# A hybrid of scans, convolutions, attention and expert mixtures on one core: experts' outputs added by way of ScalarE and GpSimd, decays issued two at a time

## The chip, the core and the metric

The kernel runs on one core of a Trainium2 chip. The core has five engines that each work through their own instructions in order: TensorE (PE in the profile) for matrix products, VectorE (DVE), ScalarE (ACT), GpSimd (POOL), and SyncE (SP), which here issues DMAs. Engines wait for each other through semaphores. The metric is the time of one execution on the device in microseconds (us); lower is better.

## What is computed

Four layers work on an input of 4 images of 32x32 positions (1,024 positions) and 256 channels. Layer 0 is a convolution and then a state-space scan with 512 channels of 64 states; layer 1 is a small residual convolution block; layer 2 is masked attention and a mixture of 8 experts; layer 3 is a second scan, with 512 channels of 16 states, and a second mixture of 8 experts. Cut to the parts that the change touches:

```python
# the scans, layers 0 and 3: for each image, channel and state, over the positions
dA = jnp.exp(dtt[:, :, None] * A)
h = dA * h + (dtt * xt)[:, :, None] * Bt[:, None, :]
y = jnp.einsum('bdn,bn->bd', h, Ct)

# the mixture of layer 2 (hidden size 256; layer 3 has 512 and no residual inside)
for e in range(E):
    h = jax.nn.gelu(tokens @ w1[e] + b1[e], approximate=False)
    y = h @ w2[e] + b2[e]
    out = out + combine[:, e:e + 1] * y
```

`combine` holds each token's weights for the experts; it is zero but for the best two. All eight experts are computed for all tokens.

## The kernel before

Two streams of work are interleaved as the program is written. One is the list of scans (`scans`, line 378). A scan of one image is cut into units: one unit is 128 rows (pairs of a channel and a state) by 1,024 positions. Layer 0 has 256 units for an image and layer 3 has 64, so there are 1,280 units, in the order of the list `SCANS` (line 31): (layer 0, image 0), (0,1), (3,0), (0,2), (3,1), (0,3), (3,2), (3,3).

For unit k these steps run:

- `load` (line 460): a DMA broadcasts the step sizes into a tile dA; there are five such tiles.
- `decay` (line 473): ScalarE turns dA into exp(scale x dA) in place, with the row's A as the scale.
- `first` (line 483): two matmuls spread the inputs into a PSUM tile ps_rep, of which there are two.
- VectorE multiplies ps_rep by B in place (line 542), and then runs the scan over the positions into a tile h (line 546).
- GpSimd multiplies h by C (line 547).
- `pair` (line 498): TensorE sums over the states of two units into ps_y.

In the loop at line 533, `load` runs four units ahead, `decay` two and `first` one.

The other stream is the side work: stages named `front` (the start of layer 0), `middle` (the end of layer 0, layers 1 and 2, and the start of layer 3) and `last` (the end of layer 3), one of each for each image. They are generators that give up control after each small step. After each half of a unit the loop in `run` (line 607) lets up to two side steps go. It stops when the clock of some engine has passed that of VectorE: the kernel keeps a clock for each engine, and adds an estimate for every instruction that it writes (`Metered`, line 96). So side work is written beside as many scan units as it takes VectorE's clock to follow. A stage also waits where it needs the result of a scan. The other way round, a scan needs what a stage makes: where that isn't there five units before the scan begins, `need` (line 556) writes out all that is missing at once. The last scan, (3,3), begins at unit 1216, and its inputs come from the last `middle`, so what is left of that stage at unit 1211 comes in one block that no scan stands beside.

The mixture is `moe` (line 582). Its items run through `pipe` (line 194), which gives each item its first step at one tick and its second step at the next. Items are of two kinds. An "h" item multiplies tokens by a part of the first weights into a PSUM tile ps_h, and ScalarE applies the gelu with a bias into h_m, one tick later. An "o" item multiplies h_m by the second weights into a PSUM tile ps_e for two blocks of 128 tokens, and one tick later VectorE adds the result, scaled by the token's weight, to the running sum tb: two `scalar_tensor_tensor` of 128x256 for an item, 32 items and so 64 instructions for a mixture. The PSUM tiles of the side work, ps_h and ps_e among them, share three buffers in turn (`ps`, line 188). The gelu and the exponential of a decay lie in different tables of ScalarE, and each switch is an instruction of its own, ACT_TABLE_LOAD.

Attention (`heads`, line 449) goes in 64 steps for an image: scores into PSUM, their exponentials on ScalarE into p, and the products with the values. In the block that no scan stands beside, the scores go to the scans' free PSUM tiles under the name ps_sx.

Line 128 in the profile is the helper of `Metered` that writes most instructions, so groups are told apart there by their tiles.

Of the kernel before, what the change touches and what calls it, by code (L numbers as in the profile page):

```python
# [7 lines left out]
F32 = mybir.dt.float32  # L8
BF16 = mybir.dt.bfloat16
I32 = mybir.dt.int32  # L10
AF = mybir.ActivationFunctionType
ALU = mybir.AluOpType
# [4 lines left out]
P = 128  # L17
NB = 4
L = 1024
TB = L // P  # L20
C = 256
# [115 lines left out]
class Hybrid:  # L137
# [240 lines left out]
    def scans(self, mp, psum):  # L378
# [7 lines left out]
        nc = self.nc  # L386
# [10 lines left out]
        y = None  # L397
# [44 lines left out]
        def chunks_ahead(k, late=False):  # L442

            if not late and k + AHEAD < len(units) and units[k + AHEAD][2:] == (0, 0, 0):
                waiting.append(k + AHEAD)
            while waiting:
                scan, d = units[waiting[0]][:2]
                if ("parts", *scan, d) not in self.ready:  # L450
                    if waiting[0] - k > LATEST:
                        break
                    if not late:
                        return True
                    self.alone = True
                chunk(waiting.pop(0))
                self.alone = False
            return False

        def load(k):  # L460
            if k >= len(units):
                return
            scan, d, c, i, j = units[k]
            n = self.states[scan[0]]
            G = P // n
            a = mp.tile([P, L], F32, tag="dA", name="dA", bufs=5)
            r = 64 * c + 32 * j + G * i
            nc.sync.dma_start(
                a, self.mem["dt", *scan, d][r : r + G, :].unsqueeze(0).to_broadcast([n, G, L])
            )  # L470
            state[k] = a

        def decay(k):
            if k >= len(units):
                return
            scan, d, c, i, j = units[k]
            G = P // self.states[scan[0]]
            col = (d * P + 64 * c + 32 * j) // G + i
            nc.scalar.activation(
                state[k], state[k], AF.Exp, scale=self.tables[scan[0]][0][:, col : col + 1]  # L480
            )

        def first(k):
            if k >= len(units):
                return
            scan, d, c, i, j = units[k]
            spread = self.tables[scan[0]][1]
            G = P // self.states[scan[0]]
            ps = psum.tile([P, L], F32, tag="x", name="ps_rep", bufs=2)
            for g in range(2):  # L490
                cols = slice(g * 512, (g + 1) * 512)
                nc.tensor.matmul(
                    ps[:, cols], lhsT=spread[:, i, :], rhs=chunks[scan, d][:, 2 * c + j, cols],
                    start=True, stop=True,
                )
            state[k] = (state[k], ps)

        def pair(k):

            nonlocal y  # L500
            scan, d, c, i, j = units[k]
            n = self.states[scan[0]]
            per = 32 * n // P
            collect = self.tables[scan[0]][2]
            if i == 0:
                y = psum.tile([P, 512], F32, tag="y", name="ps_y", bufs=1)
            h = [state.pop(k - 1), state.pop(k)]
            for g in range(2):
                for j in range(2):
                    at = 32 * (2 * g + j)  # L510
                    nc.tensor.matmul(
                        y[at : at + 32, :], lhsT=collect[:, i, :],
                        rhs=h[j][:, g * 512 : (g + 1) * 512],
                        start=(i == 0), stop=(i == per - 1), tile_position=(0, at),
                    )
            if i == per - 1:
                yo = mp.tile([P, 512], F32, tag="yo", name="yo", bufs=2)
                nc.scalar.copy(yo, y)
                to = self.keep(("y", *scan, d, c), [64, L])
                for g in range(2):  # L520
                    nc.sync.dma_start(to[:, g * 512 : (g + 1) * 512], yo[64 * g : 64 * g + 64, :])
                if c == 1:
                    self.done.add((scan, d))
# [4 lines left out]
        for k in range(2, 4):  # L528
            load(k)
        decay(0)  # L530
        decay(1)
        first(0)
        for k in range(len(units) + 4):
            waits = chunks_ahead(k)
            load(k + 4)
            if not waits:
                first(k + 1)
            decay(k + 2)
            if k < len(units):
                a, inp = state.pop(k)  # L540
                B, Cm = rows[units[k][0]]
                nc.vector.tensor_tensor(inp, inp, B, ALU.mult)
            yield
            if k < len(units):
                h = mp.tile([P, L], F32, tag="h", name="h", bufs=5)
                nc.vector.tensor_tensor_scan(h, a, inp, 0.0, ALU.mult, ALU.add)
                nc.gpsimd.tensor_tensor(h, h, Cm, ALU.mult)
                state[k] = h
            if k % 2 == 1 and 2 <= k < len(units) + 2:
                pair(k - 2)  # L550
            if waits:
                chunks_ahead(k, True)
                first(k + 1)
            yield
# [1027 lines left out]
    def moe(self, which, b, tb):  # L1582

        nc, tc, a = self.nc, self.tc, self.a
# [5 lines left out]
        with tc.tile_pool(name=f"m{which}{b}", bufs=1, side="right") as op:  # L1590
            xT = op.tile([P, 2, L], F32, name="xTm")
            cw = op.tile([P, TB, NEXP], F32, name="cw")
# [9 lines left out]
            with tc.tile_pool(name=f"mg{which}{b}", bufs=1, side="right") as gp:  # L1602
# [4 lines left out]
                ps = self.ps("ps_lg", (P, TB, NEXP))  # L1607
# [14 lines left out]
                if which == 2:  # L1622
                    for j in range(0, TB, 2):
                        tj = tb[:, j : j + 2, :]
# [15 lines left out]
                got = {}  # L1640
# [13 lines left out]

                yield from self.pipe(range(TB // 2), last, add, cost=1.0)

            hidden_of = {}
            got = {}

# [24 lines left out]
            def two(item):  # L1684
                kind, e, g, i = item
                if kind == "h":
                    nc.scalar.activation(
                        hidden_of[e, g][:, i, :], got.pop(item), AF.Gelu,
                        bias=b1[:, e * KH + i : e * KH + i + 1],
                    )  # L1690
                    return
                ps = got.pop(item)
                for s in range(2):
                    m = 4 * g + 2 * i + s
                    nc.vector.scalar_tensor_tensor(
                        tb[:, m, :], ps[:, s, :], cw[:, m, e : e + 1], tb[:, m, :],
                        ALU.mult, ALU.add,
                    )

            items = []  # L1700
            blocks = [(e, g) for e in range(NEXP) for g in range(2)]
            for n in range(len(blocks) + 1):
                if n < len(blocks):
                    items += [("h", *blocks[n], i) for i in range(KH)]
                if n:
                    items += [("o", *blocks[n - 1], i) for i in range(2)]
            yield from self.pipe(items, one, two, cost=2.6 if which == 2 else 3.4)

    def route(self, gp, lg, cw, renorm):

# [296 lines left out]
```

## Time and profile before

| what | value |
|---|---|
| time, median of 3 runs | 6460.27 us (6456.73 to 6466.56) |
| the profiled execution: time | 6467.21 us |
| the profiled execution: span from first to last instruction | 6465.4 us |
| mean TensorE clock granted | 0.825 |

```profile
PE 5210.1 (81%) x20249; PEld 2107.8 (33%) x20249; DVE 5153.1 (80%) x4328; ACT 3408.1 (53%) x4075; POOL 3648.4 (56%) x1796
```

The line gives each engine's busy time, its share of the span, and its instructions; PEld is TensorE's loading of weights, which overlaps its products. These are averages over stretches of very different kinds. The largest groups of ScalarE and GpSimd, and ScalarE's table loads, follow. A row has the line, engine, operation and tiles, the shapes, the count, then busy time and mean ns of one, and then the engine's idle time ahead of these instructions with what ended most of it.

```profile
L128 POOL TENSOR_TENSOR h<-h,rows 128x1024 f32<-128x1024 f32 x1280 | 3026.7, 2367 | 1816.9 <-DVE h L128 1567.0
L128 ACT ACTIVATE dA<-dA,A_L_conv_A_log 128x1024 f32<-128x1024 f32 x1024 | 1147.7, 1144 | 616.5 <-DMA dA<-dt 575.9
L128 ACT ACT_TABLE_LOAD x483 | 619.7, 1283 | 58.4 <-PE ps_h L128 43.1
L128 ACT ACTIVATE h_m<-ps_h,cols 128x512 f32<-128x512 f32 x384 | 260.2, 687 | 507.7 <-PE ps_h L128 505.2
```

A further 95 table loads stand under line 266, which makes 578.

### The profile page before, as it was taken

The page shows a single profiled execution, that of the slowest core. Times are in us where ns is not written, and L with a number is a line of the kernel's source. Part 1 is how long each engine was busy: PE and PEld are TensorE (multiplying, and loading weights), DVE is VectorE, ACT ScalarE, POOL GpSimd, SP SyncE. Part 2 cuts the span into 40 slices and gives each one's busy share as a digit, 9 for nine tenths or more (in the row PEclk, how much of TensorE's full clock was granted, in tenths as well). Part 3 has the DMA queues.
Part 4 walks back from the last instruction along what each step waited for, and adds up shares of the span by engine and source line. Part 5 has one row for each costly group of instructions (what it writes and reads, how often), then busy time and mean ns, then how long its engine had stood idle before and what let it go on. Part 6 is the DMA issues. An engine that isn't in the chain of part 4 may idle for free. (4 is left out here: it accounts for less than half of the span.)

```text
span 6465.4 us, 59678 instructions
## 1 busy us (share of the span) xinstructions
PE 5210.1 (81%) x20249; PEld 2107.8 (33%) x20249; DVE 5153.1 (80%) x4328; ACT 3408.1 (53%) x4075; POOL 3648.4 (56%) x1796
## 2 busy tenths in 40 slices
PE   6677685689797579989689689798699688968979
PEld 2222130222342022243245232253254222524656
DVE  5888989988898998899889988898899981258311
ACT  3565664355576335567568445477387353246311
POOL 2797868665557666555856665557756661065100
PEclk7677695689797579989789689798699788978979
DMA  3555546443355566345644665354555750156221
GB/s 114 162 158 174 176 154 198 158 147 116 125 182 174 169 163 163 114 137 178 193 150 165 189 158 142 107 168 163 178 169 168 193 146 7 53 154 159 64 69 33
DMA packets 347995, 935.77 MB, mean 145 GB/s; under 512 B 37444, under 2 KB 119952, under 8 KB 346064
## 3 DMA queue, kind: packets, MB, share of 16 engines
q1 hardware_dynamic: 345248, 929.36, 47.2%
q0 software_dynamic: 2128, 2.13, 0.2%
q8 instruction: 166, 2.72, 0.2%
q14 instruction: 165, 1.35, 0.1%
q10 hardware_dynamic: 288, 0.20, 0.0%
HBM read 841.81 MB, written 93.16 MB: 145 GB/s over the span
## 5 line engine op out<-in xcount | busy, mean ns | idle before, releaser
L128 POOL TENSOR_TENSOR h<-h,rows 128x1024 f32<-128x1024 f32 x1280 | 3026.7, 2367 | 1816.9 <-DVE h L128 1567.0
L128 DVE TENSOR_TENSOR_SCAN h<-dA,ps_rep 128x1024 f32<-128x1024 f32 x1280 | 2923.0, 2284 | 142.8 <-ACT dA L128 12.8
L128 DVE TENSOR_TENSOR ps_rep<-ps_rep,rows 128x1024 f32<-128x1024 f32 x1280 | 1550.9, 1212 | 182.6 <-PE ps_rep L128 178.4
L128 ACT ACTIVATE dA<-dA,A_L_conv_A_log 128x1024 f32<-128x1024 f32 x1024 | 1147.7, 1144 | 616.5 <-DMA dA<-dt 575.9
L128 PE MATMUL ps_rep<-S,spread_L_conv_A_log 96*128 96x512 bf16 x2048 | 770.4, 465 | 840.8 <-DVE h L128 791.1
L128 PE MATMUL ps_y<-h,collect_L_conv_A_log 128*32 128x512 f32 x4096 | 739.5, 773 | 14.6 <-POOL h L128 14.6
L128 PE MATMUL ps_h<-xTm,we 128*128 128x512 f32 x1536 | 716.5, 606 | 0.0
L128 PE MATMUL ps_e<-we,h_m 128*128 128x256 f32 x3072 | 701.2, 381 | 2.5 <-ACT h_m L128 1.7
L128 PEld LDWEIGHTS <-spread_L_conv_A_log 96*128 96x128 bf16 x2048 | 159.3, 103 | 1651.4 <-DVE h L128 1348.1
L128 ACT ACT_TABLE_LOAD x483 | 619.7, 1283 | 58.4 <-PE ps_h L128 43.1
L128 PEld LDWEIGHTS ps_e<-we,h_m 128*128 128x128 f32 x3072 | 579.2, 190 | 153.6 <-issue 62.7
L128 DVE SCALAR_TENSOR_TENSOR tb<-ps_e,cw,tb 128x256 f32<-128x256 f32 x512 | 220.1, 474 | 410.6 <-PE ps_e L128 410.5
L128 ACT ACTIVATE h_m<-ps_h,cols 128x512 f32<-128x512 f32 x384 | 260.2, 687 | 507.7 <-PE ps_h L128 505.2
L128 ACT ACTIVATE p<-ps_sc 128x512 f32<-128x512 f32 x432 | 234.4, 595 | 382.8 <-PE ps_sc L128 381.9
L128 PEld LDWEIGHTS ps_h<-xTm,we 128*128 128x128 f32 x1536 | 292.4, 193 | 333.4 <-issue 287.8
L128 ACT ACTIVATE dA<-dA,A_L_attn_A_log 128x1024 f32<-128x1024 f32 x256 | 290.6, 1146 | 198.3 <-DMA dA<-dt 168.8
L128 PE MATMUL ps_rep<-S,spread_L_attn_A_log 96*128 96x512 bf16 x512 | 182.7, 444 | 178.6 <-DVE h L128 167.7
L128 PE MATMUL ps_at<-p,v 128*32 128x512 f32 x1024 | 276.6, 621 | 0.9 <-ACT sums L128 0.7
L128 PE MATMUL ps_at<-p,ones 128*32 128x512 f32 x1024 | 276.5, 620 | 0.0
L128 PE MATMUL ps_sc<-qT,kT 32*128 32x512 f32 x864 | 262.6, 665 | 14.8 <-ACTq L1382 8.8
L128 POOL TENSOR_TENSOR sp_l<-sp_l,sp_e 128x512 f32<-128x512 f32 x62 | 78.4, 1265 | 272.4 <-DVE sp_e L128 250.5
L128 PE MATMUL ps_cv<-pad,diag 128*128 128x512 f32 x504 | 230.9, 599 | 0.0
(333 smaller groups left out, 4926.2 us busy)
## 6 DMA issues: line engine op xcount, KB each, us to landing
dA<-dt SPq DMA_DIRECT2D x1280, 512.0 KB
we<-in_L_ffn_W_dram SPq DMA_DIRECT2D x64, 512.0 KB
parts<-parts SPq DMA_DIRECT2D x62, 384.0 KB
S<-parts SPq DMA_DIRECT2D x93, 256.0 KB
dt<-sp_r SPq DMA_DIRECT2D x64, 256.0 KB
y<-yo SPq DMA_DIRECT2D x128, 128.0 KB
y_back<-y SPq DMA_DIRECT2D x64, 256.0 KB
we<-in_L_ffn_w_dram SPq DMA_DIRECT2D x64, 256.0 KB
```

What stands on the lines that cost most here:

```text
L128: return got(*args, **kw)
```

## The change

In five of the eight mixtures, those of layer 2 for images 0 to 2 and those of layer 3 for images 0 and 1, the addition of an expert's output is done in two steps. ScalarE scales each 128x256 half out of PSUM into a new tile y_m in SBUF (two buffers), and at the next tick of `pipe` GpSimd adds the whole 128x512 tile to tb. The three mixtures that are left keep the addition on VectorE. The price that is given to `pipe` for a tick stays the same.

In the loop over units, the decays of units k+1 and k+2 are written together at each even k, ahead of `first`; before, the decay of unit k+2 was written at each k, behind `first`.

```diff
         decay(0)
-        decay(1)
         first(0)
         for k in range(len(units) + 4):
             waits = chunks_ahead(k)
             load(k + 4)
+            if k % 2 == 0:
+                decay(k + 1)
+                decay(k + 2)
             if not waits:
                 first(k + 1)
-            decay(k + 2)
...
+            beside = b < (NB - 1 if which == 2 else NB - 2)
             hidden_of = {}
             got = {}
...
                 ps = got.pop(item)
+                if beside:
+                    got[item] = y = op.tile([P, 2, C], F32, tag="ym", name="y_m", bufs=2)
                 for s in range(2):
                     m = 4 * g + 2 * i + s
+                    if beside:
+                        nc.scalar.activation(y[:, s, :], ps[:, s, :], AF.Copy, scale=cw[:, m, e : e + 1])
+                        continue
                     nc.vector.scalar_tensor_tensor(
                         tb[:, m, :], ps[:, s, :], cw[:, m, e : e + 1], tb[:, m, :],
                         ALU.mult, ALU.add,
                     )
+
+            def three(item):
+                kind, e, g, i = item
+                if kind == "h":
+                    return
+                m = 4 * g + 2 * i
+                tj = tb[:, m : m + 2, :]
+                nc.gpsimd.tensor_tensor(tj, tj, got.pop(item), ALU.add)
...
-            yield from self.pipe(items, one, two, cost=2.6 if which == 2 else 3.4)
+            steps = (one, two, three) if beside else (one, two)
+            yield from self.pipe(items, *steps, cost=2.6 if which == 2 else 3.4)
```

## The prediction

> **What bounds the kernel now.** I read the page's 40 slices first, then busy time by stretch, VectorE's groups and waits, and the order of VectorE and ScalarE inside a mixture. Durations are of the profiled execution (6467.2 us, span 6465.4), which lies 7 us above the median of 6460.3; I sum against it and subtract those 7 at the end.
>
> ```profile
> DVE  5888989988898998899889988898899981258311
> PEclk7677695689797579989789689798699788978979
> ```
>
> For 33 of 40 slices VectorE is 80 to 100% busy; then it falls to 1 and 2. By stretch (the first and fourth rows are mixtures of layer 2 and layer 3 beside full scans, then attention beside scans, almost pure scan, the solo burst, and all until the burst):
>
> ```profile
> core 0: us, PE busy (x) PEld busy (x) DVE busy (x) ACT busy (x) POOL busy (x), PEclk, DMA share, GB/s
> 1718.00:1872.00 154.00, 150.27 (x600) 81.38 (x598) 145.37 (x140) 122.15 (x116) 82.52 (x35) 0.98 0.47 151
> ...
> 3293.00:3609.00 316.00, 307.87 (x1258) 163.99 (x1257) 300.53 (x226) 260.27 (x246) 190.59 (x81) 0.99 0.49 162
> ...
> 1302.00:1718.00 416.00, 352.68 (x1756) 106.48 (x1757) 354.26 (x293) 211.79 (x302) 241.49 (x114) 0.85 0.38 126
> 2083.00:2351.00 268.00, 157.65 (x528) 34.34 (x521) 257.64 (x175) 83.57 (x77) 175.66 (x76) 0.56 0.59 176
> 5331.00:5695.00 364.00, 329.73 (x1324) 154.99 (x1322) 64.88 (x170) 116.56 (x162) 20.89 (x16) 0.92 0.09 30
> 0.00:5331.00 5331.00, 4230.32 (x16643) 1572.61 (x16645) 4755.41 (x3780) 3010.62 (x3569) 3397.96 (x1657) 0.81 0.52 159
> ```
>
> Up to 5331 us the scan's VectorE work sets the pace: one unit is a multiply and a scan, and in the timeline of a plain stretch a unit returns every 3.54 us (2199, 2202.5, 2206.0). The mixtures are nearly balanced: VectorE 95%, TensorE 97%, ScalarE 80%. That matters, since the change only relieves the first. VectorE's groups until 5331:
>
> ```profile
> L128 DVE TENSOR_TENSOR_SCAN h<-dA,ps_rep 128x1024 f32<-128x1024 f32 x1212 | 2767.8, 2284 | 135.4 <-ACT dA L128 11.2 <-DVE ps_rep L128 3.4 <-DVEq L1382 1.0
> L128 DVE TENSOR_TENSOR ps_rep<-ps_rep,rows 128x1024 f32<-128x1024 f32 x1212 | 1468.6, 1212 | 173.8 <-PE ps_rep L128 169.6
> L128 DVE SCALAR_TENSOR_TENSOR tb<-ps_e,cw,tb 128x256 f32<-128x256 f32 x320 | 136.2, 471 | 14.7 <-PE ps_e L128 14.6
> ```
>
> Decays are hardly ever late (11 us), and exactly 320 expert additions lie here. From 5331 VectorE idles because the last scan, (3,3), needs layer 2 and front of image 3. That is the solo burst: TensorE paces it, with an attention step every 2.81 us (rows of ScalarE's timeline):
>
> ```profile
> 5344.78 1.02 ACT L128 ACTIVATE p<-ps_sx 128x1024 f32<-128x1024 f32 x1 [1.78 <-PE ps_sx L128]
> 5347.59 1.02 ACT L128 ACTIVATE p<-ps_sx 128x1024 f32<-128x1024 f32 x1 [1.78 <-PE ps_sx L128]
> ```
>
> After 6025 us TensorE alone runs the last mixtures, which keep the old code.
>
> **What the Trainium skill says.** "ScalarE: Activation LUTs", What ACT_TABLE_LOAD costs, gives 1.28 us for a load, about 1.38 us of drain on top, and 186 ns plus 0.833 ns an element for an ACTIVATE, plus 93 ns for each pointer operand. The trace has the same load, 1283 ns, but no drain: at 3331.45 a load follows an ACTIVATE that ended at 3331.43, and the next ACTIVATE starts at 3332.74. I use 1.28. "GPSIMD Engine Reference", 4.1 Engine selection, says that GpSimd has no PSUM port and adds two tensors about half as fast as VectorE: hence ScalarE's copy to SBUF first; here 128x512 takes 1264 to 1275 ns on GpSimd. "SBUF — State Buffer", SBUF: two separate sides, says that GpSimd and a VectorE operation with two SBUF inputs lock each other out. The trace agrees: VectorE's sp_x, with two SBUF inputs, takes 691 to 2731 ns. A scan unit has one input in PSUM, and its durations (1.21, 2.29) are the same everywhere, so more GpSimd work should not slow it.
>
> **The change, part by part.**
>
> Removed from VectorE: 5 of 8 mixtures (layer 2 of images 0 to 2, layer 3 of images 0 and 1), 64 additions each, 320. They are the 320 above: 136 us busy, and 14 us of waits for ps_e. Gain 150 us if nothing takes their place.
>
> Added to ScalarE: 320 scaled copies of 128x256 from PSUM. No row has this form; 128x512 with one pointer takes 687 ns, 128x128 390 ns. The skill's price is 186+213+93 = 492 ns, or 399 where neighbours overlap. I take 490: 157 us.
>
> Table loads: the order in which the changed kernel's ScalarE instructions stand has 471 loads, that of before 578. 107 x 1.283 = 137 us back. But unevenly: a layer-2 mixture goes from 48 to 40 loads, a layer-3 one from 98 to 66.
>
> Added to GpSimd: 160 additions of 128x512, 160 x 1.27 = 203 us. In a layer-2 mixture that is 82.5 + 32x1.27 + 10.5 units x 2.37 = 148 of 163 us. High, but off the path. Each addition is a new wait on GpSimd: it waits for two ScalarE copies, and behind it stand the scan's multiplications by C, and behind these TensorE's ps_y. A pair's ps_y is issued two units (7.1 us) after its second scan, and the multiplication takes 2.4 of them, so an addition of 1.27 us and a wait of some 3 us fit: cost nothing; without that room each would hold TensorE.
>
> What moves: the kernel's planner lets side work run only as its clock for VectorE advances. With the additions gone a mixture now spreads over more scan units: by the order of instructions 45 for 34.5, and 91.5 for 81. No TensorE work goes. So the gain is that 52 more units (10 or 11 in each mixture) pass beside mixtures, and each mixture itself gets longer.
>
> Layer 2, from the 154 us: VectorE 154 - 27 - 1 + 10.5x3.55 = 163; TensorE 150.3 + 10.5x1.17 = 163 (1.17 us a unit: ps_rep 20.9 and ps_y 20.0 us for 35 units there); ScalarE 122.2 - 10.3 + 31.4 + 10.5x1.145 = 155. Three engines at 95 to 100%. TensorE was idle 2.5%; keeping that gives 167, a loss of 4. Layer 3: VectorE 322, TensorE 320, with the same idle 328, a loss of 6; ScalarE 260 - 41 + 31 + 12 = 262, easy. Loss 3x4 + 2x6 = 24 us.
>
> The burst: the side stages are later against the scan units. Attention of image 3 starts at unit 1189.5 instead of 1173, and the burst is still forced at 1211. So 58 attention steps are left for it (exps from ps_sx in the order) and not 40: 18 x 2.81 = 51 us more. In return some attention beside scans goes, where VectorE idles 62 of 416 us for 64 steps: 18 steps fewer save perhaps 10, an estimate.
>
> Decays two at a time: the odd unit's decay now comes one unit later. I took each odd unit's decay behind the ScalarE operation that stands before the next unit's decay, added one load where that has one, and compared with the start of its scan. The slack, median 5 to 10 us now, falls to 4.4 in layer-2 mixtures, 3.0 in layer 3 and 1.4 in attention; it is negative 76 times of 640, 38 us together. I take half, 20: stalls let the other engines catch up. Bounds 0 and 40. The unbroken block on ScalarE grows by 1.14 us; what comes behind it in attention is later by 13 us in all for 64 steps, since ScalarE waits there anyway. A decay issues no DMA, and no queue but ScalarE's changes by the move: the load of dA stays four units ahead.
>
> Front, pure scans, burst layout and tail are else unchanged, at nothing.
>
> Sum: -150 + 24 + 51 - 10 + 20 = -65. 6467 - 65 = 6402, less 7: **6395 us**.
>
> **Rivals.**
>
> *Clean.* VectorE remains the sole bound: losses of the mixtures and the decays 0, so -150 + 51 - 10 = -109: 6351. For it: VectorE waits for decays only 11 us. Against: TensorE at 97% in the mixtures.
>
> *ScalarE takes over layer 2.* It waited 30 us in such a mixture (28 of it for ps_h) and would keep these waits: 155 + 30 = 185 instead of 167, 3 x 18 = 54: -11, 6449. For it: a gelu cannot start before its matmul. Against: part of these waits are only being early.
>
> *Slower: ScalarE's blocks stop TensorE.* The expert outputs' PSUM buffers, three in rotation, are now freed by ScalarE, behind a block of load, two decays, load (4.85 us, 3.71 before). TensorE works in order, so a held ps_h or ps_e keeps the next ps_rep, and so the scan. 252 loads in the five mixtures make 126 blocks. If the stop is the added decay's 1.14 us each, 144 us: -65 + 144 = +79, 6539. It decides from 78/126 = 0.6 us a block. Against: TensorE now waits for ScalarE 0.3 us in a whole layer-3 mixture, though gelus stand behind such blocks already.
>
> That the pairing spares no loads is ruled out by the order.
>
> **How the numbers follow.** Forecast 0.50, clean 0.22, ScalarE in layer 2 0.14, slower 0.14. The forecast's own range, from decays at 0 or 40 and mixture losses of 0 to 60, is 6351 to 6451. Range 6335 to 6475: it takes in clean and the ScalarE case. About 0.2%, 13 us, is what a measurement tells from no change. The ScalarE case lies at its edge, so I split it: faster 0.77, same 0.09, slower 0.14.
>
> **What would show it.** Right: 192 additions left on VectorE, 471 loads, scan units in mixtures at 3.6 to 3.7 us, the burst starting about 115 us earlier and lasting some 50 longer, tail alike. Wrong: scans waiting on dA by over 50 us; TensorE waiting for y_m or h_m; mixtures at over 3.9 us a unit; two-input GpSimd additions stretching the scan.

## The result, and the profile after

| what | before | changed |
|---|---|---|
| median of 5 runs | 6460.27 us (6456.73 to 6466.56) | 6405.39 us (6397.51 to 6429.18) |
| ratio, with its 95% interval | | 0.992 (0.9899 to 0.9941) |
| the profiled execution: time, span | 6467.21, 6465.4 us | 6403.18, 6401.5 us |

The change makes the kernel 55 us faster in the medians and 64 us in the two profiled executions; 6395 was predicted. The page's slices of the changed kernel, VectorE and TensorE's clock:

```profile
DVE  5888889988898998899889988898999841258311
PEclk7677695689799579989779889798699788978979
```

The picture is the same: VectorE leads until it falls, but the fall begins one slice earlier. Now a 4 stands ahead of the 1, where an 8 stood before. Busy time by stretch, here for the mixtures (three of layer 2, then one of layer 3) and for the first 363 us of the solo burst. After the stretch and its length each engine has its busy time and its instructions:

```profile
core 0: us, PE busy (x) PEld busy (x) DVE busy (x) ACT busy (x) POOL busy (x), PEclk, DMA share, GB/s
1722.00:1887.00 165.00, 160.02 (x660) 83.55 (x658) 155.50 (x96) 146.41 (x183) 140.60 (x76) 0.99 0.53 172
2784.00:2948.00 164.00, 159.58 (x659) 83.21 (x657) 154.53 (x94) 145.82 (x181) 140.00 (x75) 0.99 0.53 171
4153.00:4317.00 164.00, 159.39 (x658) 82.99 (x657) 154.55 (x93) 146.62 (x183) 140.17 (x75) 0.99 0.52 168
3283.00:3609.00 326.00, 315.81 (x1315) 166.65 (x1318) 310.59 (x183) 250.71 (x286) 248.59 (x121) 1.00 0.56 178
...
5213.00:5576.00 363.00, 328.28 (x1502) 145.12 (x1499) 70.23 (x172) 122.62 (x164) 22.45 (x17) 0.92 0.08 26
```

A mixture of layer 2 now takes 164.5 us where it took 154, and one of layer 3 takes 326 where it took 316. They got longer, and the kernel got faster: between these times stand 45 and 91 scan units, where there were 35 and 81. (The prediction counted by the order of the instructions, which gives up to half a unit more or less: 45 for 34.5, 91.5 for 81.) TensorE and VectorE are busy for 94 to 97% of them. VectorE's groups until the burst begins at 5213 us:

```profile
L128 DVE TENSOR_TENSOR_SCAN h<-dA,ps_rep 128x1024 f32<-128x1024 f32 x1212 | 2768.3, 2284 | 168.3 <-ACT dA L128 42.9 <-DVEq L1383 1.7 <-POOL h L128 1.5
L128 DVE TENSOR_TENSOR ps_rep<-ps_rep,rows 128x1024 f32<-128x1024 f32 x1212 | 1466.2, 1210 | 137.2 <-PE ps_rep L128 136.3
```

The expert additions have left this part: 192 of 512 are left, after it. The scan keeps its 2284 ns, with 160 additions of 1.27 us more on GpSimd. Scans wait for decays 43 us, where they waited 11. What took the additions' place, in the groups of ScalarE (first two rows; another 95 table loads stand under line 266, 471 in all, as forecast) and in the view of the tile y_m (its GpSimd row, with least, median and greatest duration):

```profile
L128 ACT ACT_TABLE_LOAD x376 | 482.4, 1283 | 10.2 <-DMA dA<-dt 3.5
L128 ACT ACTIVATE y_m<-ps_e,cw 128x256 f32<-128x256 f32 x320 | 130.9, 467 | 67.6 <-PE ps_e L128 48.4 <-POOL tb L128 17.1 <-POOL h L128 2.1
```

```profile
L128 POOL TENSOR_TENSOR tb<-tb,y_m x160: 1252/1272/1297, 1737.3 to 4980.5; 128x512 f32<-128x512 f32 x160
```

Where the time went can be read at three scans whose starts both traces show. All are worked out from the rows of the scans in the traces:

```
                                          before    changed   difference
start of unit 1152 ((0,3) is done)        5072.0     4939.1     -132.9
start of unit 1211 (the solo burst)       5328.3     5212.7     -115.6
span                                      6465.4     6401.5      -63.9
from unit 1152 to the end                 1393.4     1462.3      +68.9
```

Until unit 1152 the kernel gains 133 us. From there on it loses 69 us of them again: the side work is later against the scans (at unit 1152 the changed kernel still has 11 units of its fifth mixture to go), and more of it is left for a part that VectorE doesn't bound.

### The profile page after: what moved, and what is told of

Its sections match the earlier page's. It is cut to its first block, busy times and chain, and to the rows that moved or that the text cites. A ratio compares the mean times of both kernels' runs of the same rounds, so it can differ in the third digit from the quotient of the medians.

```text
span 6401.5 us, 59819 instructions
## 1 busy us (share of the span) xinstructions
PE 5176.6 (81%) x20249; PEld 2119.0 (33%) x20249; DVE 5032.9 (79%) x4008; ACT 3379.0 (53%) x4270; POOL 3834.3 (60%) x1956
## 5 line engine op out<-in xcount | busy, mean ns | idle before, releaser
L128 DVE TENSOR_TENSOR_SCAN h<-dA,ps_rep 128x1024 f32<-128x1024 f32 x1280 | 2923.7, 2284 | 176.2 <-ACT dA L128 43.5
L128 PE MATMUL ps_rep<-S,spread_L_conv_A_log 96*128 96x512 bf16 x2048 | 751.7, 456 | 768.7 <-DVE h L128 720.6
L128 ACT ACTIVATE dA<-dA,A_L_conv_A_log 128x1024 f32<-128x1024 f32 x1024 | 1125.2, 1142 | 435.8 <-DMA dA<-dt 385.2
L128 PE MATMUL ps_y<-h,collect_L_conv_A_log 128*32 128x512 f32 x4096 | 703.3, 742 | 13.7 <-POOL h L128 13.7
L128 ACT ACT_TABLE_LOAD x376 | 482.4, 1283 | 10.2 <-DMA dA<-dt 3.5
L128 DVE SCALAR_TENSOR_TENSOR tb<-ps_e,cw,tb 128x256 f32<-128x256 f32 x192 | 83.8, 478 | 395.8 <-PE ps_e L128 395.8
L128 ACT ACTIVATE p<-ps_sc 128x512 f32<-128x512 f32 x396 | 214.9, 595 | 316.9 <-PE ps_sc L128 306.5
L128 POOL TENSOR_TENSOR sp_l<-sp_l,sp_e 128x512 f32<-128x512 f32 x62 | 78.4, 1265 | 285.9 <-DVE sp_e L128 259.3
L128 PE MATMUL ps_sc<-qT,kT 32*128 32x512 f32 x792 | 241.4, 659 | 4.0 <-ACT p L128 1.8
```

The lines of the kernel that those rows point to most:

```text
L128: return got(*args, **kw)
```

## The experiments

Ratios are to the kernel before, each with its 95% interval. Figures of stages come from one profiled execution of each kernel. "Over the pace" below means a stretch's time less 3.545 us for each of its scan units, which is what a unit takes in plain scans; units are counted from the start of one scan to the start of another.

**The mixtures without the pairs (e1).** The changed kernel, with the loop's decays as they were:

```diff
+        decay(1)
         first(0)
...
-            if k % 2 == 0:
-                decay(k + 1)
-                decay(k + 2)
             if not waits:
                 first(k + 1)
+            decay(k + 2)
```

> The mixtures of the changed kernel, with the decays issued as before (one at a time, two units ahead). The mixtures keep their places (45 or 46 units for layer 2, 91.5 for layer 3), and 56 attention steps are left for the solo burst. Table loads: 48 to 52 in a layer-2 mixture instead of 41, 98 in a layer-3 one instead of 65. My theory: ScalarE stays just below its limit in layer 2 (146 + 8 x 1.28 = 156 of 164.5 us), so a mixture of layer 2 takes 165 to 169 us and one of layer 3 326 to 331, +20 in all, and the late decays go (43 us of scans waiting for dA back to about 11), -30: 6390 to 6410, as the changed kernel. Rival (the pairing is what makes the mixtures pay, since ScalarE would be the bound of layer 2): layer-2 mixtures at 175 us or more and a time of 6430 or more.

Measured: 6390.82 us (6387.03 to 6398.06), ratio 0.9891 (0.9876 to 0.9907). By stretch, its first layer-2 mixture (46 scan units) and its first of layer 3 (91):

```profile
1717.70:1887.50 169.80, 162.56 (x671) 83.53 (x669) 158.94 (x98) 155.11 (x189) 143.39 (x76) 0.99 0.53 169
3290.20:3619.80 329.60, 318.09 (x1319) 166.30 (x1318) 310.91 (x183) 292.58 (x317) 249.15 (x121) 0.99 0.55 176
```

The time lies in the expected range and the rival falls: with ScalarE (the fourth engine of the row) busy 155 of 170 us, 91%, the mixture is 6.8 us over the pace, against 5.0 in the changed kernel. The mixtures alone bring all of the gain, and more. The sum behind the expectation is another matter: the five mixtures together cost 10 us more than in the changed kernel, not 20, and where the late decays cost time is taken up with e5 to e8.

**The pairs without the mixtures (e2).** The kernel before, with the loop of the changed kernel.

> The kernel before with the decays issued two at a time and nothing else. Table loads 443 instead of 578. My theory: ScalarE bounds nothing here, so 173 us of loads saved buy nothing, and odd decays come late: scans wait for dA some 20 to 40 us more, time 6460 to 6485. Rival (fewer loads on ScalarE free TensorE's PSUM buffers earlier and so shorten mixtures and attention): 6445 or less.

Measured: 6467.36 us (6445.89 to 6480.76), ratio 1.0009 (1.0 to 1.0018). 135 table loads of 1.283 us fewer, 173 us of ScalarE's time, bought nothing in the whole. The mixtures hardly changed: from TensorE's first product to the last addition image 0's took 150.4 us in layer 2 (149.1 before) and 313.5 in layer 3 (315.0). The scans' wait for dA rose. These rows are from the views of VectorE's waits, before and then with the pairs (total, number, longest):

```profile
DVE h L128 <- ACT dA L128: 12.8, 7, 5.7
```

```profile
DVE h L128 <- ACT dA L128: 49.0, 74, 3.6
```

A few long waits have become 74 short ones, mean 0.66 us, nearly all at odd units, whose decays now lead by one unit and no longer by two. The neutral whole is a balance, though. Unit 210 begins at 1058.8 us, 16 later than before (1042.7); from there to unit 1152 e2 takes 4011.2 us, 18 less (4029.4). It is the three stretches with attention that are shorter, by 8.9, 7.6 and 6.4 us over the pace. So e2 doesn't show that fewer loads are worth nothing in every stage, only that this loop as a whole gains nothing.

**The new mixtures at the old places (e3).** VectorE is relieved, but the planner is told otherwise: after the copies and additions its clocks are set to what the old additions would have made of them.

```diff
                 if beside:
+                    clock = dict(self.clock)
+                    clock["vector"] += 2 * 0.444
                     got[item] = y = op.tile([P, 2, C], F32, tag="ym", name="y_m", bufs=2)
...
+                if beside:
+                    self.clock.update(clock)
...
+                clock = dict(self.clock)
                 nc.gpsimd.tensor_tensor(tj, tj, got.pop(item), ALU.add)
+                self.clock.update(clock)
```

> The changed kernel, with the planner's clocks charged in the mixtures as for the additions on VectorE (0.444 us each, nothing for ScalarE and GpSimd), so that every mixture stands beside the same scan units as in the run with the pairing alone: 34.5 units for layer 2, 81 for layer 3, 41 attention steps in the solo burst. To be compared with e2_pair_only. My theory: the gain comes from the units that pass beside a mixture, not from the relief of VectorE itself; with the old places TensorE paces the mixtures, at 150 us for layer 2 (154 before) and 308 to 311 for layer 3 (316): only 15 to 30 us below e2_pair_only. Rival (the relief of VectorE pays directly, 136 us of additions gone): 100 us or more below e2_pair_only.

Measured: 6442.14 us (6434.48 to 6465.97), ratio 0.9967 (0.9955 to 0.9979): 25 us below e2 in the medians (the profiled execution is the slowest of six). The first 34 units of a layer-2 mixture took 147 us (151 in e2), and the 81 of one of layer 3 304 (315). By stretch, a layer-2 and a layer-3 mixture of e3:

```profile
1743.00:1890.00 147.00, 144.95 (x571) 77.96 (x571) 118.44 (x69) 123.55 (x158) 112.73 (x62) 0.98 0.47 152
3324.00:3628.00 304.00, 304.00 (x1259) 165.13 (x1258) 278.57 (x163) 237.71 (x275) 227.12 (x112) 1.00 0.52 169
```

and VectorE's multiplication in the first of the two:

```profile
L128 DVE TENSOR_TENSOR ps_rep<-ps_rep,rows 128x1024 f32<-128x1024 f32 x34 | 41.6, 1223 | 23.2 <-PE ps_rep L128 23.1
```

VectorE is busy 118 of 147 us and waits 23 for TensorE, which is busy for all but 2. So the relief by itself is worth 4 to 11 us a mixture, and then TensorE is the bound. The large gain comes only when the planner puts 10 more scan units beside each mixture. The rival, 100 us or more from the relief itself, is refuted.

**Letting the late side work run ahead (e4).** The changed kernel, without the limit of VectorE's clock from unit 1152 on:

```diff
+                    lead = LEAD if n < 2 * 1152 else 1000.0
-                    if max(clock.values()) > clock["vector"] + LEAD or self.advance() is None:
+                    if max(clock.values()) > clock["vector"] + lead or self.advance() is None:
```

> The changed kernel, with side work let run ahead of VectorE's clock without limit from unit 1152 on (two steps after each half unit). By the order of instructions 15 attention steps are left for the solo burst instead of 58, the burst ends within 2 units after unit 1211, and the last mixture of image 2 is done at unit 1254.5. My theory (the solo burst is a cost of the late side work, 2.81 us a step): 43 x 2.81 = 121 us of burst go, some of it comes back as scans waiting for ps_rep: 6320 to 6370. Rival (TensorE paces everything from unit 1152 on, so moving its work about gains nothing): within 20 us of the changed kernel.

Measured: 6445.71 us (6427.99 to 6459.1), ratio 0.9976 (0.9968 to 0.9983): slower than the changed kernel by 40 us, so my expectation was a miss, and the rival's 20 us too. The solo burst did shrink: from the start of unit 1211 to that of unit 1212, between which it lies, it took 354 us instead of 450, 96 less where 121 were expected. But from unit 1152 to the end it took 1486 us, against 1462 in the changed kernel. VectorE's waits from 4980 us on show part of the return:

```profile
DVE tb L128 <- PE ps_e L128: 415.1, 96, 19.7
...
DVE ps_rep L128 <- PE ps_rep L128: 67.5, 24, 10.1
```

The wait for ps_rep was 24.1 us in the same part of the changed kernel. The mixture of layer 3, image 2, now took 247 us for 24 scan units (260 for 31 in the changed kernel). The burst's length is therefore not a cost that was saved by starting its work earlier inside this part; that the side work left at unit 1152 is what counts fits this, but no run varied it alone. In the two profiled executions e4 is 52 us behind: 24 of them after unit 1152, and 29 before it (4967.7 us there, 4939.1 in the changed kernel), where both kernels' instructions stand in the same order.

**Pairs only in the mixtures (e5, and once more as e10), the changed kernel again (e6), the mixtures alone again (e8).** e5 tracks the last decay written:

```diff
-            if k % 2 == 0:
-                decay(k + 1)
-                decay(k + 2)
+            while decayed < (k + 1 if self.mixing and k % 2 else k + 2):
+                decayed += 1
+                decay(decayed)
...
+            self.mixing = True
             yield from self.pipe(items, *steps, cost=2.6 if which == 2 else 3.4)
+            self.mixing = False
```

> The changed kernel with the decays in pairs only while a mixture's experts are written, and one at a time, two units ahead, everywhere else. Places of the mixtures as with the mixtures alone; table loads 472; 38 to 42 loads in a layer-2 mixture, 62 to 66 in a layer-3 one. Theory from the two traces (changed kernel against mixtures alone): the pairing saves 5.4 us in a layer-2 mixture (164.5 against 169.9) and 2.5 in a layer-3 one, 21 in all, and loses about as much or more in the stages of ScalarE-bound latency around them (layer 3's front 215 against 211.7 us). So pairs in the mixtures alone give about 20 us below the mixtures alone: 6365 to 6380. Rival (these differences of a few us in a stage are the scatter of executions and not the pairing): within 8 us of e8_mix_again.

> The changed kernel as it is, beside the other three on the same chip. Theory (the pairing costs 7 to 15 us): above e8_mix_again by 7 to 15 us. Rival (pairing is neutral): within 5 us of it.

> The mixtures alone once more, beside the changed kernel and e5 on the same chip: 6385 to 6397 as in e1_mix_only, if that time was no accident of that chip.

Measured on one chip: e6 6411.83 us, ratio 0.993 (0.9916 to 0.9943); e8 6391.03, ratio 0.9899 (0.9884 to 0.9914); e5 6380.34, ratio 0.9875 (0.986 to 0.989). So the loop with pairs costs the changed kernel 21 us, more than the 7 to 15 that I then expected: the intervals of e6 and e8 just miss each other. e5 is 11 us below e8, half of what was expected, and its interval overlaps that of e8 slightly. On another chip, as e10, it took 6382.08 us, ratio 0.9881 (0.9864 to 0.9897). It is the fastest version found, 78 us below the kernel before on both chips and some 31 us below the changed one (e6, same chip). In the traces a layer-2 mixture is 4.3 to 5.0 us over the pace in e5, against 6.7 to 6.8 in e8 and 5.0 in the changed kernel: pairs save some 2 us in each. (The 5.4 us of the expectation set 45 scan units against 46.) Scans wait for dA 14 us in e10 and 47 in e6.

The starts of scans show where the 21 us go. The times of all profiled executions with the five new mixtures at their new places, with the kernel before and e2 below them:

```
                                       start of     from there to
                                       unit 210     unit 1152
decays singly     e1, e8               1042, 1036   3895, 3891
pairs in mixtures e5, e10              1037, 1041   3890, 3879
... and attention e9                   1041         3898
pairs everywhere  changed, e6          1053, 1065   3887, 3888
                  e7, e4               1059, 1062   3893, 3905
decays singly     before               1043         4029
pairs everywhere  e2                   1059         4011
```

Up to unit 210 no mixture of experts and no attention has begun. There the kernels with pairs everywhere are 21 us slower in the mean, and no execution of one kind (1036 to 1043) comes near the other (1053 to 1066, with e3). From unit 210 to 1152 pairs make no difference beyond the scatter. VectorE's waits up to unit 210, in e8 and then in e6:

```profile
DVE sp_e L128 <- ACT sp_l L128: 17.8, 5, 5.3
DVE sp_x L128 <- ACT parts L128: 15.4, 10, 3.0
...
DVE h L128 <- ACT dA L128: 9.9, 3, 5.8
```

```profile
DVE sp_e L128 <- ACT sp_l L128: 27.3, 5, 11.5
DVE sp_x L128 <- ACT parts L128: 20.2, 12, 3.9
DVE h L128 <- ACT dA L128: 17.1, 15, 3.8
```

The wait for decays is 7 us longer, and that for the side steps sp_e and sp_x, in which the front of a layer makes the scans' step sizes and inputs, 14 us. From unit 210 to 1152, e8 and then e6:

```profile
DVE ps_rep L128 <- PE ps_rep L128: 103.9, 89, 7.7
...
DVE h L128 <- ACT dA L128: 2.1, 2, 1.6
```

```profile
DVE ps_rep L128 <- PE ps_rep L128: 85.6, 80, 5.4
DVE h L128 <- ACT dA L128: 28.0, 46, 1.9
```

Here the scans wait 26 us more for decays, and 18 us less for TensorE's ps_rep. The loop with pairs also shifts the planner's clocks, and with them the places of the side work: image 0's first mixture begins beside unit 369 in e6, 367.7 in e8. Whether the 21 us at the start come from late decays or from these places is not settled; no run had the pairs at the start alone.

**All eight mixtures in the new form (e7).**

```diff
-            beside = b < (NB - 1 if which == 2 else NB - 2)
+            beside = True
```

> The changed kernel with all eight mixtures in the new form, so also that in the solo burst (layer 2 of image 3) and the two at the end. Everything up to unit 1211 is written in the same order. Theory: TensorE paces these three and hides VectorE's additions (idle 396 us before them, waiting for ps_e), so the move gains nothing; the last output has to go through ScalarE (0.9 us for two copies) and GpSimd (1.3) instead of 0.9 on VectorE: 0 to +5 us against e6_changed_again. Rival (the third step and ScalarE's load hold TensorE where no scan hides it): the burst's mixture takes over 115 us instead of 110, +15 us or more.

Measured: 6423.88 us (6414.25 to 6434.33), ratio 0.9945 (0.9931 to 0.9959), 12 us above e6, more than the 0 to 5 expected. The two intervals overlap, so the size is unsure, but no gain is to be seen. The rival falls at its own mark: the burst's mixture took 112.9 us from TensorE's first product to its last, 112.5 in e6. The chain of waits at the end of image 2's mixture shows the longer path that was expected (start, duration, engine and tile):

```profile
6099.95 13.83 PE ps_e L128 x64
6114.84 1.27 POOL tb L128
6116.13 4.43 DMA out_dram<-tb
```

In e6 the output's DMA starts 0.9 us after the last ps_e; here it starts 2.4 us after it. That is 1.4 us of the 12. After the last product of the last mixture this kernel runs another 8.9 us, e6 6.7: 2.2 more. The rest was not traced to one cause.

**Pairs in the mixtures and in attention (e9, beside e10).**

```diff
+                self.mixing = True
                 yield from self.all_heads(fp, tb, qT, kT, v, maskT, mT, xa, wo)
+                self.mixing = False
```

> As e5 (pairs in the mixtures' experts), and pairs also while attention's heads are written. Table loads stay 472, places stay. Theory from the traces: over the pace of plain scans (3.545 us a unit), attention of images 0 and 1 costs 86 and 88 us in the changed kernel and 94 and 97 with single decays, so pairs in the heads gain about 9 us in each of these two: 10 to 20 us below e10. Rival (the gain there comes from the other places that the changed kernel's attention has, 92 units for 90.5, and not from the pairs): within 6 us of e10, and a slack of odd decays in attention of 1.4 us that turns into scans waiting for dA.

> e5 as it is, beside e9 on the same chip: 6373 to 6387, as in e5.

Measured: e9 6394.44 us, ratio 0.9897 (0.9881 to 0.9914), 12 us above e10. The expectation was a miss, and the reverse holds in all three attentions: 99.7, 100.1 and 88.0 us over the pace, against 97.9, 96.3 and 78.4 in e10. Scans waited 35 us for dA instead of 14. This is where the slack of odd decays was smallest. The 9 us that attention of images 0 and 1 saves in the changed kernel (11 with units counted as here) therefore comes from something else, its other places perhaps: e2, with the new loop and the old mixtures, saves 7 us in each too. That stays open.

## Why the prediction was right

The median came out 10 us above the forecast; the profiled executions differ by 64 us, where the sum was 65. Two terms make up the result, the mixtures and the burst, and both came as they were worked out. That the rest fits to the microsecond is luck: it is a balance of pieces that were forecast at nothing, or elsewhere. From the scans of the two profiled executions, over the pace, in us:

```
                                                  forecast   measured
the five mixtures                                  -126       -124.5
from the start to unit 210                            0         +9.9
stretches with attention, images 0 to 2               0        -23.3
fronts of layer 3 between mixtures                    0        +12.0
from the fifth mixture to unit 1211                 -10        +10.2
unit 1211 to unit 1222, with the solo burst         +51        +50.3
from unit 1222 to the end                             0         +1.4
late decays, in mixtures and attention              +20     (in the rows above)
sum                                                 -65        -63.9
```

- *The mixtures, -150 + 24 = -126.* The five fell by 24.9, 24.0, 25.3, 25.4 and 24.8 us. The balance of three engines was read rightly: 167 us were forecast for layer 2 and 328 for layer 3, 164.5 and 326 came, and e3 shows that TensorE would be the bound next. Two slips in the sums did no harm: by the working for layer 2 VectorE's 322 in layer 3 would be 326, still below the 328; and the trace has 50 more units where 52 were counted, but then the mixtures came out 1.5 to 2.5 us shorter than forecast. ScalarE's copy takes 467 ns (490 was taken), and GpSimd's addition 1272 ns (1270).
- *The burst, +51.* Unit 1211 begins 115.6 us earlier (about 115 was forecast), and from there to unit 1222, where the scans run on, it takes 498 us instead of 448: +50. The order has 58 solo attention steps, as it said. e4 adds what the prediction did not see: this is no price of the solo burst as such, since moving 43 steps out of it gained nothing.
- *Attention, -10.* This term is wrong: the part of image 3's attention beside scans costs about the same (30.8 and 29.6 us over the pace). The attentions of images 0 and 1 became cheaper by 11 us each. The cause is open; it goes with the loop and not with the mixtures, since e2 has 7 us of it in each and e8 none.
- *Decays, +20, between 0 and 40.* The size is right by luck. e6 against e8 gives 21 us, but they are lost before unit 210, and the prediction had them in the mixtures and attention, which come later. There the decays are late as it said, 26 us of waits more, but the time doesn't grow (3888 us from unit 210 to 1152 in e6, 3891 in e8). That "stalls let the other engines catch up" for all of it, and not for half, would explain this; the places of the side work differ too, so it is not shown.
- *Neutral stages.* "At nothing" was not so. The first 210 units took 10 us more in the changed kernel and 23 in e6, the same program, and layer 3's fronts 5 to 7 us each.

Of the signs of being wrong, one did show: in the whole execution TensorE's weight loads waited 27 us for y_m, and 51 for h_m where they waited 7 before. But its products were idle for only 35 us of the five mixtures, so these stops cannot have been the 144 of the slower rival.

Of the rivals, the clean case (6351) failed in the mixtures, where 25 of the 150 us were lost with TensorE at 97%. ScalarE as the bound of layer 2 (6449) is refuted by e1, where it carried 9 us more work in such a mixture and cost about 2 over the pace. The slower case, ScalarE's blocks stopping TensorE at 0.6 us each, would have needed mixtures at over 3.9 us a unit: they run at 3.66 and 3.59.

## What to carry to other kernels

Where two streams of work are interleaved and one engine paces one of them, taking work off that engine doesn't shorten the stage: it lets more of the other stream pass beside it. So ask what the planner will put there, which engine is next (here TensorE, two to three per cent away), and what side work is late at the end in return; half of the gain of 133 us was given back there. 135 fewer table loads on an engine that was not the bound did not shorten this kernel. Issuing work in pairs to save them takes half of it its lead and moves the other stream's work too; find by stretch where that costs time. Here it was in the first 210 units, and not where the lead was shortest.

## What the runs showed of the hardware that was not expected

- Loads of ScalarE's tables stand back to back with their ACTIVATEs, 1283 ns each; 135 fewer of them left the time of the whole kernel as it was (e2).
- VectorE's scan (one input in SBUF, one in PSUM) takes 2284 ns before and after, though GpSimd makes 160 additions of 1.27 us more beside it.
- Kernels with the same order of instructions up to a point reach it at different times: unit 1152 begins at 4939.1 us in the changed kernel, at 4953.4 in e6, the same program, and at 4967.7 in e4. Most of a stage's time repeats to a tenth (image 0's layer-2 mixture is 5.0 us over the pace in all four kernels with that order), while attention and the layer-0 fronts vary: attention of image 2 is 89.0, 89.1, 89.1 and 104.2 us over the pace in the changed kernel, e6, e7 and e4. A difference of 15 us between two single executions of this kernel says nothing yet.
